# Selective-scan image kernel: the last stage of an image placed inside the next image's attention, x kept raw and updated in place, v computed in three row bands

## The chip, the cores and the metric

The kernel runs on one core of one Trainium2 chip. The metric is device time in microseconds (us) of the whole launch. Before the change three runs took 21485.61, 21488.65 and 21491.22 us; the median is 21488.65 us. All values are 32-bit floats.

## The reference, cut to what matters

Eight images of 384 channels by 64x64 pixels pass through two residual layers. Layer 0 is channel attention on a group-normalized input, layer 1 a four-direction selective scan with a token layer norm and a gelu.

```
xn   = group_norm(x)                                # 32 groups of 12 channels
q,k,v = dwconv3x3(conv1x1(xn, w*), dw*)             # 1x1 mix of channels, then a 3x3 depthwise filter
attn = softmax(l2norm(q) @ l2norm(k).T * temp)      # 8 heads of 48 channels, over the 4096 pixels
x    = x + conv1x1(attn @ v, wproj)
y    = selective_scan(group_norm(x))                # 4 directions, state of 16 per channel
x    = x + gelu(layer_norm_over_channels(y) * ln_w + ln_b)
```

## The kernel before, in words

Channels lie on the 128 partitions, in NJ = 3 blocks (j or m); the 4096 pixels of a row lie in the free dimension, in eight chunks of 512. One loop over the images (L789) calls three functions in turn; each opens its own pools of on-chip memory and closes them.

**channel_attention (L138).** Three tiles xn of 128x4096 are loaded (L153), their statistics taken (L168) and turned into mean and rstd per channel by norm_factors (L103: two groups of one-column matmuls and a few tiny vector operations). VectorE then normalizes xn in place (L171). conv (L175) makes one 128x4096 block of k, q or v: per chunk three accumulating matmuls into a PSUM tile pc of three buffers (L182), a ScalarE copy into pre (L186), then one ScalarE multiply by the centre tap (L187) and eight VectorE multiply-adds, one per other tap (L197), each over the whole block. pre and acc have two buffers each. inverse_norm (L203) squares a block with its sum on ScalarE (L205), then a square root and two tiny vector operations. to_tokens (L211) turns a block into tokens by matmuls against the identity (L215; for k against diag(1/norm), so that k is scaled on the way) and ScalarE copies (L219). q's tokens are multiplied with k's into pa (L246), from which the logits (L251), softmax (L255 to L260) and the merged matrix mT = attention times wproj (L267, L271) follow. v (L273) shares its memory with kT. When all of v stands, 24 blocks of 128x512 are projected (L287), added to x, which is loaded a second time (L282, L292), measured for the next group norm (L293) and stored to x1d in DRAM (L294).

**selective_scan (L297).** After norm_factors and a normalization in place (L336 on ScalarE, L341 on VectorE) it runs 32 steps of 8 periods each. In a period VectorE runs six scans (L481), GpSimd two products (L469), ScalarE exponentials (L462) and copies (L515), TensorE transposes and sums (L503, L538, L544); B comes by DMA (L416), three periods ahead. All of these are pinned to their written order. The sums go to y in DRAM (yd, L570, L589).

**finish (L746).** All of y is loaded as tokens (L756) and measured (L762, L763), normalized on VectorE (L771), transposed back (L779), passed through gelu (L782), added to x1 on GpSimd (L786, xr loaded at L769) and stored (L787). o and xr have two buffers.

What is not pinned is ordered by a scheduler when the program is built: it fixes one static order for each engine and for each queue of DMA issues, by program order and expected readiness. Each engine works through its own order strictly. A tile tag with n buffers makes the tile n allocations later wait until the earlier one has been read for the last time. The PSUM pool ps_m of the attention has one buffer, tag "misc".

Of the kernel before, what the change touches and what calls it, by code (L numbers as in the profile page):

```python
# [9 lines left out]
F32 = mybir.dt.float32  # L10
AF = mybir.ActivationFunctionType
# [4 lines left out]
P = 128  # L16
# [18 lines left out]
PX = 4  # L35
GN_EPS = 1e-5
# [35 lines left out]
def tile_channel_attention_then_selective_scan(ctx: ExitStack, tc: tile.TileContext, a: dict):  # L72
# [12 lines left out]
    nc.vector.tensor_add(pair, twos[:, :, 0], twos[:, :, 1])  # L85
    eps = const.tile([P, 1], F32, name="eps")
# [16 lines left out]
    def norm_factors(pool, psum, stats, tag, bank):  # L103

        avg = pool.tile([P, NJ, C], F32, name=f"avg{tag}")
# [32 lines left out]
    def channel_attention(b):  # L138

        with ExitStack() as st:  # L140
# [7 lines left out]
            xn = []  # L148
            for j in range(NJ):
                t = big.tile([P, L], F32, tag="x", bufs=NJ, name=f"xn{b}_{j}")  # L150
                for h in range(2):
                    eng = nc.sync if h == 0 else nc.scalar
                    eng.dma_start(t[:, bass.ts(h, L // 2)], x_d[b, j, :, bass.ts(h, L // 2)])  # L153
                xn.append(t)
            wts, dws = {}, {}
            for n in ("wk", "wq", "wv", "wproj"):
                wts[n] = wp.tile([P, NJ, C], F32, name=f"{n}{b}")
                nc.sync.dma_start(wts[n], a[n].rearrange("(j p) o -> p j o", p=P))
            for n in ("dwk", "dwq", "dwv"):
                dws[n] = wp.tile([P, NJ, 9], F32, name=f"{n}{b}")  # L160
                nc.scalar.dma_start(dws[n], a[n])
            mask = wp.tile([P, NJ, BW], F32, name=f"mask{b}")
            nc.scalar.dma_start(mask, a["mask"])

            stats = wp.tile([P, NJ, NCH, nc.vector.BN_STATS_DIM], F32, name=f"st0{b}")
            for j in range(NJ):
                for c in range(NCH):
                    nc.vector.bn_stats(stats[:, j, c, :], xn[j][:, bass.ts(c, CH)])  # L168
            mean, rstd = norm_factors(wp, ps_m, stats, f"0_{b}", "misc")
            for j in range(NJ):  # L170
                nc.vector.tensor_scalar(  # L171
                    xn[j], xn[j], mean[:, j : j + 1], rstd[:, j : j + 1], ALU.subtract, ALU.mult
                )

            def conv(which, m, acc):  # L175

                wt, dw = wts["w" + which], dws["dw" + which]
                pre = work.tile([P, L], F32, tag="pre", name=f"pre{b}{which}{m}")
                for c in range(NCH):
                    pc = ps_c.tile([P, CH], F32, tag="pc", name=f"pc{b}{which}{m}_{c}")  # L180
                    for j in range(NJ):
                        nc.tensor.matmul(  # L182
                            pc, lhsT=wt[:, j, m * P : (m + 1) * P], rhs=xn[j][:, bass.ts(c, CH)],
                            start=j == 0, stop=j == NJ - 1,
                        )
                    nc.scalar.copy(pre[:, bass.ts(c, CH)], pc)  # L186
                nc.scalar.activation(acc, pre, AF.Copy, scale=dw[:, m, 4:5])  # L187
                pre3 = pre.rearrange("p (h w) -> p h w", w=W)
                acc3 = acc.rearrange("p (h w) -> p h w", w=W)
                for tap in range(9):  # L190
                    if tap == 4:
                        continue
                    dy, dx = tap // 3 - 1, tap % 3 - 1
                    y0, y1 = max(0, -dy), H - max(0, dy)
                    x0, x1 = max(0, -dx), W - max(0, dx)
                    o = acc3[:, y0:y1, x0:x1]
                    nc.vector.scalar_tensor_tensor(  # L197
                        o, pre3[:, y0 + dy : y1 + dy, x0 + dx : x1 + dx],
# [4 lines left out]
            def inverse_norm(acc, junk, tag):  # L203
                r = work.tile([P, 1], F32, tag="rn", name=f"rn{tag}")
# [6 lines left out]
            def to_tokens(acc, rhs, t4, out, tag):  # L211

                pt = ps_t.tile([P, 4, P], F32, tag="pt", name=f"pt{tag}_{t4}")
                for i in range(4):
                    nc.tensor.matmul(  # L215
                        pt[:, i, :], lhsT=acc[:, bass.ts(4 * t4 + i, P)], rhs=rhs,
                        start=True, stop=True,
                    )
                nc.scalar.copy(out, pt)  # L219

            kT = wp.tile([P, NT, C], F32, tag="kv", name=f"kT{b}")
            for m in range(NJ):
                acc = work.tile([P, L], F32, tag="acc", name=f"ak{b}{m}")
                pre = conv("k", m, acc)
                r = inverse_norm(acc, pre, f"k{b}{m}")
                diag = work.tile([P, P], F32, tag="diag", name=f"diag{b}{m}")
                nc.vector.tensor_scalar_mul(diag, ident, r)
                for t4 in range(NT // 4):
                    to_tokens(acc, diag, t4, kT[:, 4 * t4 : 4 * t4 + 4, bass.ts(m, P)], f"k{b}{m}")

            attn = wp.tile([P, NJ, C], F32, name=f"attn{b}")
            nc.gpsimd.memset(attn, 0.0)
            for m in range(NJ):
# [3 lines left out]
                pre = conv("q", m, acc)  # L237
# [3 lines left out]
                for t4 in range(NT // 4):  # L241
                    qT = work.tile([P, 4, P], F32, tag="qT", name=f"qT{b}{m}_{t4}")
                    to_tokens(acc, ident, t4, qT, f"q{b}{m}")
# [6 lines left out]
                lg = work.tile([P, BW], F32, tag="lg", name=f"lg{b}{m}")  # L250
                nc.vector.scalar_tensor_tensor(  # L251
                    lg[:, :wd], pa[:, :wd], r, mask[:, m, :wd], ALU.mult, ALU.add
# [8 lines left out]

            mT = wp.tile([P, NJ, C], F32, name=f"mT{b}")
            for j in range(NJ):
                pm = ps_a.tile([P, CH], F32, tag="pa", name=f"pmt{b}{j}")
                src = [i for i in range(NJ) if _overlaps(i, j)]
                for i in src:
                    nc.tensor.matmul(  # L267
                        pm[:, :C], lhsT=attn[:, i, bass.ts(j, P)], rhs=wts["wproj"][:, i, :],
# [5 lines left out]
            for m in range(NJ):  # L274
                conv("v", m, v[:, m, :])

            x1 = []
            x1_d = dram.tile([NJ, P, L], F32, tag="x1d", bufs=2, name=f"x1d{b}")
            stats1 = big.tile([P, NJ, NCH, nc.vector.BN_STATS_DIM], F32, tag="st1", name=f"st1{b}")
            for m in range(NJ):  # L280
# [561 lines left out]
```

## Time and profile before

| what | value |
|---|---|
| median of 3 runs | 21488.65 us |
| span of the profiled execution | 21487.3 us |
| VectorE (DVE) busy | 19284.7 us, 90% |
| TensorE (PE) busy | 19225.0 us, 89% |
| ScalarE (ACT) busy | 17613.4 us, 82% |
| GpSimd (POOL) busy | 15773.4 us, 73% |
| one image, from the end of one scan to the end of the next (image 1) | 2682.3 us |
| of it the scan | 2104.1 us |
| of it finish, attention and the start of the scan | 578.2 us |

In the profile's map of 40 equal slices each image is five slices: VectorE is over 90% busy in the three or four that are scan, 70% in the first, which holds the end of one image and the attention of the next. Idle time of an engine is shown ahead of the instruction that ended it, with the engine or transfer that released it in brackets. Times inside image 1 are given from the start of the span; its predecessor's scan ends at 2612.0 us.

### The profile page before, as it was taken

The page shows a single profiled execution, that of the slowest core. Times are in us where ns is not written, and L with a number is a line of the kernel's source. Part 1 is how long each engine was busy: PE and PEld are TensorE (multiplying, and loading weights), DVE is VectorE, ACT ScalarE, POOL GpSimd, SP SyncE. Part 2 cuts the span into 40 slices and gives each one's busy share as a digit, 9 for nine tenths or more (in the row PEclk, how much of TensorE's full clock was granted, in tenths as well). Part 3 has the DMA queues.
Part 4 walks back from the last instruction along what each step waited for, and adds up shares of the span by engine and source line. Part 5 has one row for each costly group of instructions (what it writes and reads, how often), then busy time and mean ns, then how long its engine had stood idle before and what let it go on. Part 6 is the DMA issues. An engine that isn't in the chain of part 4 may idle for free. (4 is left out here: it accounts for less than half of the span.)

```text
span 21487.3 us, 318562 instructions
## 1 busy us (share of the span) xinstructions
PE 19225.0 (89%) x118832; PEld 10739.5 (50%) x118832; DVE 19284.7 (90%) x16862; ACT 17613.4 (82%) x30794; POOL 15773.4 (73%) x7117
## 2 busy tenths in 40 slices
PE   7999879998799987999879998799987999879998
PEld 4555445554455544555445554455544555445554
DVE  7999879998799987999879998799987999879998
ACT  3999839998399983999839998399983999839998
POOL 0999809998099980999809998099980999809998
PEclk8999989999899998999989999899998999989999
DMA  1222312223122231222312223122231222312223
GB/s 50 80 91 91 115 45 80 91 91 116 43 80 90 92 117 42 80 90 91 118 41 81 90 91 118 41 81 90 91 119 41 80 90 92 119 40 81 90 92 107
DMA packets 871616, 1807.88 MB, mean 84 GB/s; under 512 B 123216, under 2 KB 512592, under 8 KB 860848
## 3 DMA queue, kind: packets, MB, share of 16 engines
q1 hardware_dynamic: 807888, 1658.85, 24.0%
q10 hardware_dynamic: 62176, 128.66, 1.7%
q8 instruction: 936, 15.34, 0.3%
q14 instruction: 616, 5.05, 0.1%
HBM read 1468.39 MB, written 318.77 MB: 83 GB/s over the span
## 5 line engine op out<-in xcount | busy, mean ns | idle before, releaser
L469 POOL TENSOR_TENSOR db<-w,B 128x1536 f32<-128x1536 f32 x4096 | 14157.7, 3464 | 393.0 <-DVE h L481 213.8
L481 DVE TENSOR_TENSOR_SCAN h<-da,ca,db 128x512 f32<-128x512 f32 x10752 | 13075.0, 1267 | 642.3 <-ACT da L462 317.1
L515 ACT ACTIVATE hc<-pt,ct 128x384 f32<-128x384 f32 x15128 | 8533.2, 580 | 438.9 <-PE pt L503 342.6
L462 ACT ACTIVATE da<-dt,neg_a 128x512 f32<-128x512 f32 x12288 | 8511.9, 696 | 112.7 <-DVE h L481 80.8
L503 PE MATMUL pt<-ident,h 128*128 128x128 f32 x49152 | 8076.3, 288 | 517.7 <-ACT hc L515 345.7
L503 PEld LDWEIGHTS pt<-ident,h 128*128 128x128 f32 x49152 | 5140.4, 141 | 5154.1 <-ACT hc L515 2548.5
L538 PE MATMUL py<-hc,pair 128*64 128x384 f32 x24576 | 5329.1, 512 | 9.1 <-DVE ys L589 9.1
L446 POOL TENSOR_TENSOR w<-x,dt 128x512 f32<-128x512 f32 x768 | 1083.7, 1412 | 3884.9 <-DMA cx<-bcd 3884.9
L544 PE MATMUL py<-hc,pair 128*64 128x128 f32 x24576 | 2114.2, 281 | 0.0
L481 DVE TENSOR_TENSOR_SCAN h<-da,db 128x512 f32<-128x512 f32 x1536 | 1814.4, 1231 | 246.6 <-ACT da L462 105.4
L538 PEld LDWEIGHTS py<-hc,pair 128*64 128x64 f32 x24576 | 1216.1, 135 | 1014.3 <-issue 944.9
L544 PEld LDWEIGHTS py<-hc,pair 128*64 128x64 f32 x24576 | 1568.5, 137 | 208.7 <-issue 130.2
L370 PE MATMUL px<-x,wx 128*44 128x128 f32 x6144 | 1477.1, 338 | 35.1 <-ACT x L336 28.9
L370 PEld LDWEIGHTS px<-x,wx 128*44 128x44 f32 x6144 | 645.5, 121 | 815.7 <-issue 750.6
L495 POOL COPY ca<-h 128x6 f32<-128x6 f32 x1792 | 345.7, 193 | 905.5 <-DVE h L481 902.1
L429 PE MATMUL pd<-xd,wdt 128*128 128x512 f32 x1536 | 780.0, 617 | 73.9 <-ACT hc L515 61.1
L517 DVE TENSOR_SCALAR hc<-pt,ct 128x384 f32<-128x384 f32 x1256 | 734.0, 600 | 54.9 <-PE pt L503 25.4
L134 ACT ACT_TABLE_LOAD x16 | 20.5, 1283 | 913.9 <-DVE rstd L133 841.7
L287 PE MATMUL pp<-v,mT 128*128 128x512 f32 x1152 | 525.4, 618 | 272.9 <-DVE v L197 272.9
L786 POOL TENSOR_TENSOR o<-o,xr 128x512 f32<-128x512 f32 x192 | 310.5, 1646 | 510.9 <-DVE y L771 385.1
L779 PE MATMUL pz<-ident,y 128*128 128x128 f32 x768 | 152.3, 374 | 474.6 <-DVE y L771 293.4
L287 PEld LDWEIGHTS pp<-v,mT 128*128 128x128 f32 x1152 | 226.4, 198 | 570.5 <-issue 532.2
(238 smaller groups left out, 11677.0 us busy)
## 6 DMA issues: line engine op xcount, KB each, us to landing
B<-bcd SPq DMA_DIRECT2D x2048, 512.0 KB
yd<-ys SPq DMA_DIRECT2D x128, 576.0 KB
ys<-yd SPq DMA_DIRECT2D x256, 288.0 KB
yd<-ys SPq DMA_DIRECT2D x256, 288.0 KB
x<-in_x SPq DMA_DIRECT2D x24, 2048.0 KB
x1d<-x ACTq DMA_DIRECT2D x192, 256.0 KB
y<-yd SPq DMA_DIRECT2D x64, 768.0 KB
xr<-x1d ACTq DMA_DIRECT2D x64, 768.0 KB
```

Of the source, the lines that this page charges most:

```text
L287: nc.tensor.matmul(pc, lhsT=mT[:, j, bass.ts(m, P)], rhs=v[:, j, bass.ts(c, CH)], start=j == 0, stop=j == NJ - 1,)
L370: pin(nc.tensor.matmul(split(pxs[s][:XR, :])[:, part, :], lhsT=wx[:, j, k, :], rhs=view(x1[j], k, c)[:, part, :], start=i == 0, stop=i == ...
L429: pin(nc.tensor.matmul(pds[j], lhsT=wdt[:, k, bass.ts(j, P)], rhs=xds[s], start=True, stop=True))
L446: pin(nc.gpsimd.tensor_mul(split(ws[s][:, j, :]), view(x1[j], k, c), split(dts[s][:, j, :])))
L462: pin(nc.scalar.activation(t, dts[s][:, j, :], AF.Exp, scale=neg_a[:, j, k, n : n + 1]))
L469: pin(nc.gpsimd.tensor_mul(t, ws[g // NP], bts[g][:, v : v + 1, :].broadcast_to([P, NJ, CH])))
L481: pin(nc.vector.tensor_tensor_scan(h, da, db, 0.0 if start else carries[s - 1][:, j, n : n + 1], ALU.mult, ALU.add,))
L503: pin(nc.tensor.transpose(t[:, bass.ts(j, P)], h2s[g][:, j, bass.ts(q, HP), :].rearrange("p l v -> p (l v)"), ident))
L515: pin(eng.activation(out, src, AF.Copy, scale=scale))
L517: pin(eng.tensor_scalar_mul(out, src, scale))
L538: pin(nc.tensor.matmul(py[f * HP : (f + 1) * HP, lb, :C], lhsT=pair, rhs=hc[:, f, :], **flags))
L544: pin(nc.tensor.matmul(py[f * HP : (f + 1) * HP, j, C:], lhsT=pair, rhs=hc[:, f, bass.ts(j, P)], **flags,))
```

## The change

- **The end of image b moves into the attention of image b+1.** finish is left for the last image alone. Its statistics become token_norm (16 loads of 256 tokens through three buffers), its rest finish_part, 16 parts of 256 tokens: one y load, one x1 load, two ScalarE operations that normalize, six transposes in the PSUM tag "pt", three gelus of 256 columns, one VectorE add of 128x768 (GpSimd has none any more), one store. A part takes a buffer of the tag "acc" (two of them), which k and q used before. Two parts are written after each block of v.
- **x is loaded by load_x**, written after the second period of the last step of the scan, and only by SP. Attention reads it raw: the weights are scaled by rstd on ScalarE, and minus weights times mean, a bias made by nine one-column matmuls into "misc", is added where ScalarE empties a chunk. xn's normalization and the second load of x are gone; the projection is added to x in place. The weights and the averaging matrix share two buffers ("wt"), so each is loaded when a buffer comes free.
- **k's first block is made in two halves of 32 rows, v in three bands of 32, 16 and 16 rows**; a band takes one more row on either side, for v an "edge" row kept from the band before. After a band is complete for all three blocks its projections are written among the next band's.
- **k's tokens are no longer scaled.** They are transposed at once; the inverse norms are spread to all partitions by a matmul of ones with diag (into "misc") as rks, and multiplied into the logits by one more VectorE operation per block of q.
- All attention DMAs, x1d's stores among them, are issued by SP.

```diff
-    def norm_factors(pool, psum, stats, tag, bank):
-        avg = pool.tile([P, NJ, C], F32, name=f"avg{tag}")
+    def norm_factors(pool, psum, stats, tag, bank, home={}):
+        avg = pool.tile([P, NJ, C], F32, name=f"avg{tag}", **home)
...
+    def load_x(b):
+        xs = []
+        for j in range(NJ):
+            t = big.tile([P, L], F32, tag="x", bufs=NJ, name=f"x{b}_{j}")
+            for h in range(2):
+                nc.sync.dma_start(t[:, bass.ts(h, L // 2)], x_d[b, j, :, bass.ts(h, L // 2)])
+            xs.append(t)
+        return xs
...
-            for j in range(NJ):
-                nc.vector.tensor_scalar(
-                    xn[j], xn[j], mean[:, j : j + 1], rstd[:, j : j + 1], ALU.subtract, ALU.mult
-                )
+            def weights(which):
+                wt = load_w("w" + which)
+                for j in range(NJ):
+                    nc.scalar.activation(wt[:, j, :], wt[:, j, :], AF.Copy, scale=rstd[:, j : j + 1])
+                pb = ps_m.tile([P, CH], F32, tag="misc", name=f"pb{b}{which}")
+                for m in range(NJ):
+                    for j in range(NJ):
+                        nc.tensor.matmul(
+                            pb[:, m : m + 1], lhsT=wt[:, j, bass.ts(m, P)], rhs=mean[:, j : j + 1],
...
+                bias = wp.tile([P, NJ], F32, name=f"bias{b}{which}")
+                nc.scalar.activation(bias, pb[:, :NJ], AF.Copy, scale=-1.0)
+                return wt, bias
...
-                    nc.scalar.copy(pre[:, bass.ts(c, CH)], pc)
-                nc.scalar.activation(acc, pre, AF.Copy, scale=dw[:, m, 4:5])
+                    nc.scalar.activation(
+                        pre[:, o : o + n], pc[:, :n], AF.Identity, bias=bias[:, m : m + 1]
+                    )
+                o = (y0 - lo) * W
+                nc.scalar.activation(
+                    out, pre[:, o : o + (y1 - y0) * W], AF.Copy, scale=dw[:, m, 4:5]
+                )
...
+            wk, bk = weights("k")
...
             for m in range(NJ):
                 acc = work.tile([P, L], F32, tag="acc", name=f"ak{b}{m}")
-                pre = conv("k", m, acc)
+                parts = (0, H // 2, H) if m == 0 else (0, H)
+                for y0, y1 in zip(parts, parts[1:]):
+                    pre = conv("k", wk, bk, m, y0, y1, acc[:, y0 * W : y1 * W])
                 r = inverse_norm(acc, pre, f"k{b}{m}")
                 diag = work.tile([P, P], F32, tag="diag", name=f"diag{b}{m}")
                 nc.vector.tensor_scalar_mul(diag, ident, r)
+                pr = ps_m.tile([P, CH], F32, tag="misc", name=f"pr{b}{m}")
+                nc.tensor.matmul(pr[:, :P], lhsT=ones, rhs=diag, start=True, stop=True)
+                nc.scalar.copy(rks[:, bass.ts(m, P)], pr[:, :P])
...
+            wq, bq = weights("q")
...
+            wv, bv = weights("v")
+            emit = None
+            if before is not None:
+                scale, shift = token_norm(b, wp, work, before[2])
+                def emit(i):
+                    t = work.tile([P, L], F32, tag="acc", name=f"fin{b}_{i}")
+                    room = [t[:, n * FT * NJ : (n + 1) * FT * NJ] for n in range(3)]
+                    finish_part(*before, i, scale, shift, room, ps_t, "pt")
...
-            for m in range(NJ):
-                conv("v", m, v[:, m, :])
...
-                t = big.tile([P, L], F32, tag="x", bufs=NJ, name=f"x1{b}_{m}")
-                nc.sync.dma_start(t, x_d[b, m])
...
+            parts = (0, H // 2, 3 * H // 4, H)
+            todo, left, edges = [], list(range(L // FT)) if emit else [], {}
+            for y0, y1 in zip(parts, parts[1:]):
+                for m in range(NJ):
+                    pre = conv("v", wv, bv, m, y0, y1, v[:, m, y0 * W : y1 * W], edges.get(m))
...
+                    if m > 0:
+                        for _ in range(min(len(todo), 6)):
+                            project_out(*todo.pop(0))
+                    for _ in range(min(len(left), 2)):
+                        emit(left.pop(0))
+                todo += [(m, c) for c in range(y0 * W // CH, y1 * W // CH) for m in range(NJ)]
+            for t in todo:
+                project_out(*t)
...
             for g in range(S * NP + 1):
                 period(g)
+                if g == (S - 1) * NP + 1 and b + 1 < B:
+                    x_next = load_x(b + 1)
...
+    def finish_part(b, x1_d, y_d, i, scale, shift, room, psum, tag):
...
+        nc.vector.tensor_add(o, o, xr)
+        nc.sync.dma_start(out_d[b, :, :, cs].rearrange("j p l -> p j l"), o)
...
+    x, before = load_x(0), None
     for b in range(B):
-        x1, x1_d, stats1 = channel_attention(b)
-        y_d = selective_scan(b, x1, stats1)
-        finish(b, x1_d, y_d)
+        x1, x1_d, stats1 = channel_attention(b, x, before)
+        y_d, x = selective_scan(b, x1, stats1)
+        before = (b, x1_d, y_d)
+    finish(*before)
```

## The prediction, on record before the changed kernel ran

> **What bounds the kernel now.** I read three views of image 1 in this order. First the table of stretches, cut at the stage borders: stretch, its length, then busy time of each engine with its instructions, PE clock, DMA share and rate.
>
> ```profile
> core 0: us, PE busy (x) PEld busy (x) DVE busy (x) ACT busy (x) POOL busy (x), PEclk, DMA share, GB/s
> 2612.00:2698.70 86.70, 18.79 (x96) 15.56 (x96) 31.30 (x98) 19.84 (x27) 38.81 (x24) 0.58 0.67 227
> 2698.70:2751.90 53.20, 34.18 (x87) 18.21 (x88) 23.09 (x36) 9.88 (x12) 1.06 (x1) 0.71 0.18 62
> 2751.90:2996.40 244.50, 203.31 (x878) 127.97 (x877) 213.61 (x80) 106.28 (x132) 0.00 (x0) 0.92 0.00 0
> 2996.40:3101.50 105.10, 47.04 (x100) 19.62 (x98) 104.64 (x26) 18.44 (x22) 0.00 (x0) 0.74 0.15 60
> 3101.50:3163.00 61.50, 59.09 (x140) 26.64 (x140) 35.06 (x53) 0.00 (x0) 0.00 (x0) 0.97 0.32 117
> 3163.00:3190.20 27.20, 15.34 (x76) 12.18 (x76) 10.56 (x29) 12.92 (x17) 7.12 (x5) 0.75 0.18 67
> 3190.20:5294.30 2104.10, 2024.77 (x13480) 1121.24 (x13480) 1992.14 (x1789) 2033.83 (x3642) 1924.44 (x861) 1.00 0.28 89
> ```
>
> The scan (last row) has four engines over 91% busy; its pinned order is untouched, so I leave its time alone. Of the other 578.2 us, DVE binds k, q (third row, 87%) and v (fourth, 99.6%), PE the projection (fifth); in finish and start (140 us) nobody is busy. Second, the timeline of DVE, for the gap before each stage (start, length, idle and releaser):
>
> ```profile
> 2698.68 14.34 DVE L168 BATCH_NORM_STATS2 st<-xn 128x6 f32<-128x512 f32 x24 [39.89 <-DMA out<-o]
> 2751.94 52.14 DVE L197 SCALAR_TENSOR_TENSOR ak<-pre1k,dwk,ak 128x3969 f32<-128x3969 f32 x12 [23.64 <-ACT ak L187]
> ...
> 2831.14 30.94 DVE L197 SCALAR_TENSOR_TENSOR ak<-pre1k,dwk,ak 128x3969 f32<-128x3969 f32 x7 [4.22 <-PE pc1q L182]
> ...
> 2992.66 0.37 DVE L251 SCALAR_TENSOR_TENSOR lg<-pa,rnq,mask 128x144 f32<-128x144 f32 x1 [12.78 <-PE pa L246]
> ...
> 3005.32 96.21 DVE L197 SCALAR_TENSOR_TENSOR v<-pre1v,dwv,v 128x3969 f32<-128x3969 f32 x22
> ```
>
> Between the first tap (2751.9) and q's last (2973.7) DVE stands only 9 us: blocks overlap. Third, the groups, for durations (busy, mean ns, idle before):
>
> ```profile
> L287 PE MATMUL pp<-v,mT 128*128 128x512 f32 x144 | 65.6, 617 | 34.0 <-DVE v L197 34.0
> L182 PE MATMUL pc1q<-xn,wq 128*128 128x512 f32 x144 | 65.2, 609 | 12.7 <-ACT pre1q L186 12.7
> L187 ACT ACTIVATE ak<-pre1k,dwk 128x4096 f32<-128x4096 f32 x3 | 11.1, 3713 | 0.1
> L205 ACT ACTIVATE pre1k<-ak 128x4096 f32<-128x4096 f32 x3 | 10.9, 3618 | 39.0 <-DVE ak L197 39.0
> L762 DVE BATCH_NORM_STATS2 fst<-y 128x6 f32<-128x384 f32 x32 | 16.1, 544 | 15.1 <-DMA xr<-x1d 12.7 <-DMA y<-yd 2.4
> ```
>
> ScalarE's copies of pc in the timeline show a chunk of a convolution every 2.57 us.
>
> **What the Trainium skill says.** "DMA: Bandwidth & Descriptors", section "Anatomy of one DMA", puts about 2 us of fixed cost on a DMA and says that waits happen on the issuing sequencer, not in the DMA engines: a store that waits for an add holds up every issue behind it on SP. The trace agrees: y's first load is issued at 2617.7, 5.7 us after yd's stores began. "ScalarE: Activation LUTs", section "Table sets: the hidden batching unit", says copy and identity are in every table set; so scaled weights and biased emptying add no table loads, only gelu among exponentials does, one per image (1283 ns each in the trace). "VectorE: DVE Perf Modes", section on the TRN2 errata, charges a fixed cost per instruction. Here 22 taps take 96.21 us, 4.373 each; by the difference of the two tap shapes (4416 less 4351 ns over 63 elements, 1.03 ns each) some 0.2 us of a tap is fixed. That prices the split taps: 2.29 us for half a block, 1.25 for a quarter.
>
> **The change part by part**, in us after the end of the preceding scan (2612.0 before). I follow the built program's static order, which is the same for images 1 to 7.
>
> *Start.* x is already loaded inside the scan before too (its last issues stand at 2602), so issue by SP alone costs nothing that I can see: at most 1 MB lies ahead of a B that is fetched three periods of 7.5 us early. Finish's 86.7 go; statistics start at 0, rstd stands at 22.5 as before, plus 1.5 for token statistics put between. Then three weight scalings at 0.47 (L271's row, 1.4), nine bias matmuls (2), four chunks and one row (11), emptying and half a centre tap (2.5): first tap at 41. Ahead of it stand 13 of 16 token statistics, 1.14 each; their loads go round three buffers at about 1.7 (estimated from a round trip of 5), and SP waits with wq for the averaging matrix's buffer, with token loads 4 to 15 queued behind it and these statistics ahead of the taps on DVE: 42 (38 to 47). Before: 139.9. **Gain 98.**
>
> *k and q.* Here the order gives back. (a) k0 takes 16 half taps, 36.6, and 3.4 of statistics: ends 82. On PE the last matmul of k1's convolution stands behind k0's second-half transposes and pr, which waits for square (3.6), root and diag: 5.3 to pr, 3 of transposes and matmul, 0.6 and 3.7 on ACT: k1 starts 13.5 later. (b) k1 and k2: 71. Then bias q: pb needs "misc", whose one buffer pr of k2 holds until rks is copied, so q's emptying waits for k2's norm; three chunks fill pc and PE stops. From k2's last tap: 6 to pr and rks, 2 transposes groups 2.2, pb 2, transposes and v's pb 6, five chunks 12.9, emptying and centre tap 4.3: **33 of idle DVE**. (c) q0 and q1: 71; q2 waits, as before, 32.6 from q0's square to its centre tap, and since q0 and q1 are now interleaved alone, DVE waits 14. (d) q2 and its small operations 36.7. Sum: 42+40+13.5+71+33+71+14+36.7 = 321; the token copies end 17.5 later as before: 338.5. Before: 379.2 (2991.2). So the idle 60.5 in place of 9, and 6 of statistics and splits, leave **41 of the 98**.
>
> *v and tail.* Before, from that point to the last statistics: 171.7. Now DVE does taps 55 + 60 = 115 (before 105), eighteen projections' adds and statistics at 1.38 (25), sixteen adds of 768 at 1.0 (0.69 for 512 from PSUM, scaled; 16), then six projections at PE's 2.57 (15 of 62). Sum with 3 for the first logits: 174. PE has about 118 in this window: conv 66, 18 projections 46, 96 transposes 32, less some 26 done ahead. Where v's third block of a band waits behind projections and part transposes, I count stalls of 2, 4, 2 and 2 us; the parts' adds have 17 us between pairs, but 7 between parts 11 and 12, where a store, a load and gelu (about 12) miss by 5, which partly overlap: 11 in all. 185, so **13 lost** (bounds 4 and 35; lower than 4 is excluded by the sum). Each store waits on SP for its add; behind it stand the next part's load and x1d's stores, and nobody waits for the latter before the scan's normalization. ACT's 65 (28 for the convolution, 20 to normalize, 22 gelus less overlap) and POOL's vacated adds do not bind. x's second load and xn's normalization are gone; the former was hidden behind v, the latter's 7 us is in the start's gain.
>
> *Sum.* Images 1 to 7: 41 - 13 = 28 each, 196. Image 0 has no parts: first tap 18.6 earlier (50 for 68.6), then the same idle, so q ends 34 later; v and tail 161 for 172: 23 lost. The last finish is divided finer, its loads doubled: 13 lost (0 to 30). -196 + 23 + 13 = -160 on the span of 21487.3: 21327; its run and the others lie within 4 us, so the median is taken as **21330 us**.
>
> **The rivals.** *A: the gaps don't open.* If a, b and c together stay at the 9 us of before, all eight images gain 51 more: 21330 - 410 = 20920. For it: before, blocks overlap. Against: "misc" and PE's fixed order. *B, slower: the two "acc" buffers.* Part i+2 loads only when part i is stored, and DVE, in order, stands at the add. Before, chunks of finish with two o buffers took 5 us each with 227 GB/s over the stage, which speaks for slow round trips. With a pair every 28 us: 10 + 7x28 + 23 = 229, 57 over 171.7; 57 - 41 = 16, times 7, plus 36: 21635. It turns the sign above some 25 us a pair; I estimate 15 to 17, hidden by taps. *C: DMA and PE together stretch v by 26*: 7x(26-41)+36 = -69: 21418. For it: parts, x1d's stores and y's second reading put five passes over 6 MB into v's 185 us (about 130 GB/s, where finish reached 227), and PE's last blocks stand between part transposes. Against: neither is near its own limit. *The change doesn't do what it says:* statistics could still wait for pools; the order puts them right behind the scan's last adds, which excludes it.
>
> **How the numbers follow.** Likeliest 0.73, A 0.10, C 0.08, B 0.09. The range, 21140 to 21460, takes gaps 25 us shorter per image below, and C and the v bound above; A and B stay out. About 0.2% (43 us) is what measurement tells from no change. Below 21446: most of the likeliest, A and most of C, 0.85; within, 0.06; slower, B and a tail, 0.09.
>
> **What would show it.** First tap about 42 after a scan; DVE idle of about 13, 33 and 14 before k1, q0 and q2, ended by ACT's centre taps; DVE busy 85% or more in v's stretch, down from 99.6%; no gap at the parts' adds over 6 us. Wrong if q0's gap is under 15 (A), or adds wait for "out" over 10 us a pair (B).

## The result, and the profile after

The changed kernel takes 21297.12 us, the median of four runs (21290.69 to 21307.95); beside it the kernel before takes 21489.94 (21485.61 to 21495.37). The ratio is 0.9911, with a 95% interval of 0.9893 to 0.9928: 193 us gained, where 160 were predicted. The profiled spans are 21288.9 and 21487.3. The period of an image, from the last addition of one scan to that of the next, fell from 2683.9 to 2649.3 on the mean of seven: 34.6 less each, 242 in all. Image 0 lost 30.7 us, the last finish 12.8. The sum is 198.4, the difference of the two spans.

First the table of stretches of image 1 of the changed kernel, cut at the end of the preceding scan (2642.7), the first tap of k, the ends of the gap before q0, the first logits of q2, the last statistics and the first step of the next scan. Columns: stretch, length, busy time of each engine with its instructions, TensorE clock, DMA share and rate.

```profile
core 0: us, PE busy (x) PEld busy (x) DVE busy (x) ACT busy (x) POOL busy (x), PEclk, DMA share, GB/s
2642.70:2691.70 49.00, 24.13 (x82) 15.90 (x83) 31.05 (x86) 9.79 (x15) 1.06 (x1) 0.65 0.61 183
2691.70:2812.20 120.50, 71.91 (x207) 36.76 (x205) 109.27 (x52) 41.45 (x52) 0.00 (x0) 0.80 0.02 7
2812.20:2848.50 36.30, 33.93 (x111) 22.91 (x112) 0.60 (x3) 17.69 (x24) 0.00 (x0) 0.72 0.00 0
2848.50:2987.70 139.20, 100.92 (x434) 67.47 (x433) 108.11 (x46) 54.45 (x72) 0.00 (x0) 0.85 0.04 12
2987.70:3161.30 173.60, 136.28 (x385) 63.52 (x383) 157.96 (x145) 73.89 (x126) 0.00 (x0) 0.90 0.43 144
3161.30:3188.90 27.60, 15.84 (x76) 12.35 (x76) 10.63 (x29) 12.91 (x17) 7.15 (x5) 0.72 0.19 67
3188.90:5292.10 2103.20, 2024.27 (x13480) 1121.46 (x13480) 1992.31 (x1789) 2034.09 (x3642) 1923.78 (x860) 1.00 0.27 89
```

The scan, in the last row, is as long as it was (2103.2 for 2104.1). Finish and start, 139.9 us together before, are now the 49.0 of the first row. The third row is new: 36.3 us in which VectorE works for 0.6. The fifth holds v, the projection and the final stage of the image before; VectorE is busy in 91% of it, and its 173.6 us stand against 170.2 for v and projection before. Next the timeline of VectorE in the same image: start, length, instruction, and in brackets the idle time before it and what ended that.

```profile
2648.32 14.34 DVE L169 BATCH_NORM_STATS2 st<-x 128x6 f32<-128x512 f32 x24 [5.65 <-DMA yd<-ys]
...
2691.66 2.25 DVE L237 SCALAR_TENSOR_TENSOR ak<-pre1k,dwk,ak 128x1953 f32<-128x1953 f32 x1 [1.88 <-ACT ak L225]
2742.28 52.15 DVE L237 SCALAR_TENSOR_TENSOR ak<-pre1k,dwk,ak 128x3969 f32<-128x3969 f32 x12 [6.56 <-ACT ak L225]
2848.53 52.14 DVE L237 SCALAR_TENSOR_TENSOR aq<-pre1q,dwq,aq 128x3969 f32<-128x3969 f32 x12 [31.46 <-ACT aq L225]
2932.28 13.19 DVE L237 SCALAR_TENSOR_TENSOR aq<-pre1q,dwq,aq 128x3969 f32<-128x3969 f32 x3 [6.10 <-ACT aq L225]
2987.66 0.31 DVE L297 TENSOR_TENSOR lg<-pa,rks 128x144 f32<-128x144 f32 x1 [13.46 <-PE pa L292]
...
3081.35 1.27 DVE L237 SCALAR_TENSOR_TENSOR v<-pre1v,dwv,v 128x1008 f32<-128x1008 f32 x1 [3.23 <-ACT v L225]
3103.87 7.74 DVE L237 SCALAR_TENSOR_TENSOR v<-pre1v,dwv,v 128x1008 f32<-128x1008 f32 x6 [3.54 <-ACT v L225]
3135.57 10.23 DVE L237 SCALAR_TENSOR_TENSOR v<-pre1v,dwv,v 128x1008 f32<-128x1008 f32 x8 [1.58 <-ACT v L225]
3148.03 0.69 DVE L343 TENSOR_TENSOR x<-x,pp 128x512 f32<-128x512 f32 x1 [2.23 <-PE pp L338]
```

The brackets count idle time since any instruction, and a norm's tiny operations break some gaps up. From last tap to first tap the three gaps are 11.7 us before k1, 36.3 before q0 and 14 before q2. The first line shows a wait that no step of the prediction has: the statistics of x start 5.65 us after the scan, when the last store of y has landed. Third, four groups of image 1 (busy time, mean ns, idle before):

```profile
L338 PE MATMUL pp<-v,mT 128*128 128x512 f32 x144 | 67.9, 623 | 14.5 <-DVE v L237 7.2 <-ACT pre1v L221 6.4 <-DVE x L343 0.9
L216 PE MATMUL pc1q<-x,wq 128*128 128x512 f32 x144 | 64.6, 603 | 0.0
...
L830 DVE BATCH_NORM_STATS2 fst<-fy 128x6 f32<-128x384 f32 x32 | 16.5, 544 | 5.1 <-DMA fy<-yd 5.1
...
L858 DVE TENSOR_TENSOR fin<-fin 128x768 f32<-128x768 f32 x16 | 15.2, 953 | 0.5 <-ACT fin L854 0.5
```

The projection's idle time fell from 34.0 to 14.5: it no longer stands behind the whole of v. Token statistics wait for loads 5.1 us where they waited 15.1, and the sixteen additions of the parts wait half a microsecond in all.

### The profile page after: what moved, and what is told of

It is laid out like the page before. It is cut to its first block, busy times and chain, and to the rows that moved or that the text cites. A ratio compares the mean times of both kernels' runs of the same rounds, so it can differ in the third digit from the quotient of the medians.

```text
span 21288.9 us, 318429 instructions
## 1 busy us (share of the span) xinstructions
PE 19267.7 (91%) x118160; PEld 10725.5 (50%) x118160; DVE 19285.1 (91%) x17190; ACT 17955.0 (84%) x31571; POOL 15456.3 (73%) x6926
## 5 line engine op out<-in xcount | busy, mean ns | idle before, releaser
L255 PE MATMUL ptk<-ident,ak 128*128 128x128 f32 x768 | 163.9, 382 | 373.2 <-DVE ak L237 336.8
L509 ACT ACTIVATE dt<-pd,dt_bias 128x512 f32<-128x512 f32 x768 | 476.2, 687 | 24.9 <-PE pd L499 21.3
L499 PEld LDWEIGHTS pd<-xd,wdt 128*128 128x128 f32 x1536 | 275.1, 192 | 388.5 <-issue 187.1
```

The costliest lines, as they stand in the source:

```text
L499: pin(nc.tensor.matmul(pds[j], lhsT=wdt[:, k, bass.ts(j, P)], rhs=xds[s], start=True, stop=True))
```

## The experiments

Each kernel was timed beside the kernel before, whose medians were 21484 to 21492 (e9 and e10 on another chip, where it was 21491.5); times are compared with the changed kernel's 21297. "After the scan" is counted from the end of image 1's preceding scan. In some images of a kernel the first tap comes 3 to 5 us later than in its other images. Image 1 is such a late image in e1 and in e4 to e10, and an early one in the changed kernel and e2. The last section says more about it.

**e1: q's bias before k.**

```diff
             wk, bk = weights("k")
+            wq, bq = weights("q")
...
-            wq, bq = weights("q")
             attn = wp.tile([P, NJ, C], F32, name=f"attn{b}")
```

> The changed kernel with one line moved: q's weights are loaded and scaled, and q's bias is made, ahead of k's blocks, so that pb of q takes the one bank of "misc" before the pr's of k's norms; all sums are the same. Theory (q0's first tap waits because pb of q stands behind pr of k2 in "misc"): the gap on VectorE before q0's first tap falls from 36 us to 4 to 12, the gaps before k1 (12) and q2 (14) stay, all eight images gain 24 to 32: 190 to 255 us under the changed kernel's 21297, so 21040 to 21105. Rival (the two "pre" buffers, or the order of the transposes on TensorE, hold q0): the gap stays at 25 or more, and the time stays within 60 us of 21297.

Measured: 21101.99 us, ratio to before 0.9823 (0.9809 to 0.9838). From the timeline of VectorE of e1, the first taps of k0 and of q0:

```profile
2679.84 2.25 DVE L237 SCALAR_TENSOR_TENSOR ak<-pre1k,dwk,ak 128x1953 f32<-128x1953 f32 x1 [7.72 <-ACT ak L225]
...
2804.93 4.35 DVE L237 SCALAR_TENSOR_TENSOR aq<-pre1q,dwq,aq 128x3969 f32<-128x3969 f32 x1 [4.49 <-ACT aq L225]
```

The gap before q0 is 4.5 us for 36.3, and the others stayed (12.2 and 14.8). So what held q0 is q's bias standing behind k's norms. That the one bank of "misc" puts it there, and not TensorE's order alone, is argued from the program: no run gave "misc" a second bank. The first tap moved from 49.0 to 56.2 after the scan in image 1 (54.0 to 54.8 in five of the other six), as q's nine bias matmuls and scalings now stand ahead of k0; so an image gains 24.

**e2: k scaled in the matmul, as before the change.**

```diff
-                    nc.tensor.transpose(pt[:, i, :], acc[:, bass.ts(4 * t4 + i, P)], ident)
+                    nc.tensor.matmul(pt[:, i, :], lhsT=acc[:, bass.ts(4 * t4 + i, P)], rhs=rhs, start=True, stop=True)
...
-                pr = ps_m.tile([P, CH], F32, tag="misc", name=f"pr{b}{m}")
-                nc.tensor.matmul(pr[:, :P], lhsT=ones, rhs=diag, start=True, stop=True)
-                nc.scalar.copy(rks[:, bass.ts(m, P)], pr[:, :P])
...
-                nc.vector.tensor_mul(lg[:, :wd], pa[:, :wd], rks[:, lo:hi])
```

> The changed kernel with one part of the change undone: k's tokens are again scaled by the diagonal in the matmul that transposes them; the ones matmul pr, the row rks and the product of the logits with it are gone. Nothing but q and v's biases then asks for "misc", and nothing of k's norms stands ahead of k1's or q0's convolution on TensorE. Theory: both gaps close, that before k1 (12 us) and that before q0 (36 us), to under 8 us each or 10 to 12 in all; 36 to 38 us in each of eight images, so about 21000 (20970 to 21030). Rival (the gap before k1 comes from k0 being made in two halves, which hold both "pre" buffers, and not from pr): only q0's gap closes, 21040 to 21105.

Measured: 21022.1 us, ratio 0.9787 (0.9773 to 0.9802). The first taps of k1 and q0 in e2:

```profile
2707.16 8.81 DVE L237 SCALAR_TENSOR_TENSOR ak<-pre1k,dwk,ak 128x3969 f32<-128x3969 f32 x2 [3.84 <-ACT ak L225]
...
2778.29 4.35 DVE L237 SCALAR_TENSOR_TENSOR aq<-pre1q,dwq,aq 128x3969 f32<-128x3969 f32 x1 [0.74 <-ACT aq L225]
```

The time is what the theory said, but not all of its parts: q0's gap is 0.7, k1's is still 8.8 us from tap to tap (its bracket shows only the piece after the norm's reciprocal), over the bound of 8. In TensorE's order of e2 no transpose stands ahead of k1's chunks any more, so something else holds k1; the rival had named the two "pre" buffers, which e9 tries. From the first logits of q2 to the last statistics e2 takes 179.7 us, 6 more than the changed kernel. The traces show where: v's taps wait 12.2 us for ScalarE in place of 9.2, the projections' additions 6.9 for TensorE in place of 4.8, the parts' additions 1.4 in place of 0.5. Image 0, without parts, takes 169.7 and 169.5. What delays ScalarE there was not tried.

**e3: the statistics' tile in another pool.**

```diff
-            stats = wp.tile([P, NJ, NCH, nc.vector.BN_STATS_DIM], F32, name=f"st0{b}")
+            stats = big.tile([P, NJ, NCH, nc.vector.BN_STATS_DIM], F32, tag="st0", name=f"st0{b}")
```

> The changed kernel with the tile of attention's first statistics in the pool of x, which lives through all images, in place of attention's own pool, whose memory was the scan's. Theory (statistics wait 5.65 us for yd's last store, because their tile lies where ys lay; and everything behind them is later by that): the wait goes, first tap 43 to 44 us after the scan in place of 49; seven images gain 5 each: 35 under 21297, about 21262. Rival (the loads of the final stage's tokens, which start behind the same store, set the first tap in any case): the wait at the statistics goes, but the waits at the tokens' statistics grow by about as much, and the time stays within 15 us of 21297.

Measured: 21344.05 us, ratio 0.9935 (0.9921 to 0.995): 47 slower, which neither expected. From the timeline of VectorE of e3, within the scan and at its end:

```profile
2533.77 0.69 DVE L169 BATCH_NORM_STATS2 st<-x 128x6 f32<-128x512 f32 x1 [0.21 <-DMA x<-in_x]
...
2554.24 1.29 DVE L169 BATCH_NORM_STATS2 st<-x 128x6 f32<-128x512 f32 x2 [1.52 <-DMA x<-in_x]
...
2664.49 0.83 DVE L113 BATCH_NORM_AGGREGATE mv<-st 128x2 f32<-128x48 f32 x3 [5.67 <-DMA yd<-ys]
```

With its memory free, the scheduler put the 24 statistics into the scan, 125 to 70 us before its end, between scan steps, where VectorE is busy for 95% of the time. The first tap comes 40.4 us after the scan, 8.6 earlier, but the period is 2656.2 for 2649.0 (mean of images 1 to 6): the scan takes 2119.0 us in place of 2103.2 in image 1, and 2101.8 in image 7, which has no next image's statistics to take in. The wait passed to the next tile of attention's own pool, mv. The late start of the statistics had kept 14.3 us of work out of an almost full engine.

**e4: no final stage in attention.**

```diff
-            if before is not None:
+            if before is not None and b < 0:
```

> The changed kernel without the final stage of images 0 to 6: their token statistics and the 16 parts are left out of the next attention, so that seven eighths of the output are not written. It prices what attention carries. The prediction counted, in the start, 13 of 16 token statistics at 1.14 us (15) ahead of the first tap, and 3 in k0 (3.4); in v, 16 us of adds and 11 of stalls; 45 us an image. Theory (the parts cost what VectorE spends on them and nothing more, since load, gelu and store are hidden): start 30 to 34 us to the first tap, v and tail 154 to 160 from the first logits of q2 in place of 173.6, so 32 to 38 us less an image: 21297 - 7 x 35 = 21050 (21030 to 21075). Rival (the parts cost more than their instructions, by the ring of two "acc" buffers, by the queue of SP or by the DMA engines that they share with the stores): v and tail under 150, an image 45 or more: under 20985.

Measured: 21277.54 us, ratio 0.9905 (0.9888 to 0.9921): 20 less than the changed kernel, where some 250 and over 310 were expected. Both fell. From the timeline of VectorE of e4, the first tap and the waits for ScalarE in v's last bands:

```profile
2701.51 4.57 DVE L237 SCALAR_TENSOR_TENSOR ak<-pre1k,dwk,ak 128x1953 f32<-128x1953 f32 x2 [22.48 <-ACT ak L225]
```

```profile
3088.25 1.27 DVE L237 SCALAR_TENSOR_TENSOR v<-pre1v,dwv,v 128x1008 f32<-128x1008 f32 x1 [5.58 <-ACT v L225]
3109.42 14.59 DVE L237 SCALAR_TENSOR_TENSOR v<-pre1v,dwv,v 128x1008 f32<-128x1008 f32 x12 [4.40 <-ACT v L225]
...
3142.14 10.23 DVE L237 SCALAR_TENSOR_TENSOR v<-pre1v,dwv,v 128x1008 f32<-128x1008 f32 x8 [5.64 <-ACT v L225]
```

Without any token statistics VectorE stands for 22.5 us from the reciprocal of rstd to the first tap in image 1, which is late (first tap at 52.2), and for 18.5 in images 3 and 4, which are early (48.3 and 48.4). In the changed kernel, with token statistics, the same way takes 18.1 to 18.6 us in its early images. So scaling, bias, chunks and centre tap take that time in any case, and the token statistics fit into it. In v the three waits are 5.6, 4.4 and 5.6 us; with the parts they were 3.2, 3.5 and 1.6. All waits of v's taps for ScalarE in image 1 add up to 17.8 us, and to 9.2 with the parts. From the first logits of q2 to the last statistics it is 169.7 us for 173.6: the 15.2 us of additions cost 4.

The difference of 20 us hides a part of the price, because five of e4's seven images are late and only one of the changed kernel's. In images 3 and 4, early in both, the period is 2641.8 and 2641.9 us for 2649.1 and 2648.8. So the parts cost 7 us an image: 4 in v and tail and 3 before the first logits of q2, where three token statistics still stand among k0's taps.

**e5: as e4, and v in one band.**

```diff
-            parts = (0, H // 2, 3 * H // 4, H)
+            parts = (0, H)
```

> The kernel of e4 (final stage of images 0 to 6 left out, seven eighths of the output not written) with v made in one band of 64 rows in place of three, so that all 24 projections come after v. It prices the bands without the parts; the comparison is with e4's 21278. Theory 1 (from the sums: taps 105 us in place of 115, but 62 of projections in place of 15 in the tail and 25 beside the taps): v and tail 167 to 174 us against e4's 169.7, because e4's taps wait for ScalarE's centre taps at each band; so within 40 us of 21278, and the bands are worth nothing by themselves. Theory 2 (the bands hide 18 projections at 2.57 us and cost 10 of taps): v and tail 195 to 210, eight images: 21480 to 21600.

Measured: 21310.81 us, ratio 0.9915 (0.99 to 0.993); v and tail take 172.5 us in image 1 and up to 174.9 in others. This is theory 1: by themselves the bands save 33 us in eight images. With the parts they leave waits in which sixteen additions find room; whether the parts would fit as well beside a single band was not tried.

**e6: six parts at a time.**

```diff
-                    for _ in range(min(len(left), 2)):
+                    for _ in range(min(len(left), 6)):
```

> The changed kernel with up to six parts of the final stage after each third of a band in place of two: the same work, but parts follow each other after some 6 us of VectorE (two to three taps and an add) in place of 17, so that the two "acc" buffers' round trip shows. Theory (the prediction's 15 to 17 us a pair, 8 a part): adds of twelve parts wait 1 to 2 us each, the last band has no parts to fill its waits (about 9 us): v and tail 173.6 + 15 to 30, and 21400 to 21510. Rival B's price (28 us a pair, 14 a part): 12 waits of 8, some 90 us an image: over 21850. Third: the round trip is shorter than 6 us: no wait over 0.5 at the adds, and only the waits in the last band come back: 21297 to 21370.

Measured: 21403.94 us, ratio 0.9959 (0.9944 to 0.9974), just within the theory's range; v and tail take 190.3 us. Six additions of parts in a row, from the timeline of VectorE of e6:

```profile
3060.93 0.96 DVE L858 TENSOR_TENSOR fin<-fin 128x768 f32<-128x768 f32 x1 [0.26 <-ACT fin L854]
3064.94 0.96 DVE L858 TENSOR_TENSOR fin<-fin 128x768 f32<-128x768 f32 x1 [0.82 <-ACT fin L854]
3075.34 0.96 DVE L858 TENSOR_TENSOR fin<-fin 128x768 f32<-128x768 f32 x1 [2.21 <-ACT fin L854]
3079.34 0.96 DVE L858 TENSOR_TENSOR fin<-fin 128x768 f32<-128x768 f32 x1
3086.73 0.95 DVE L858 TENSOR_TENSOR fin<-fin 128x768 f32<-128x768 f32 x1
3092.27 0.96 DVE L858 TENSOR_TENSOR fin<-fin 128x768 f32<-128x768 f32 x1 [2.21 <-ACT fin L854]
```

A part uses the buffer of the last but one. Where the addition waited longest, the two are 14.4 us apart (3060.93 to 3075.34) and 12.9 (3079.34 to 3092.27): that is the round trip of the two buffers, with whatever ScalarE did in between. It is half of rival B's 28 us, and under the 17 us that the prediction counted between pairs in the changed kernel, whose additions wait 0.5 us in all. The sixteen additions of e6 wait 5.6 us in all, not the 12 to 24 of its theory. The larger share of its 16.7 us is that v's taps wait 17.8 us for ScalarE again, as in e4: the last bands have no parts left to fill these waits.

**e7: e2 with k's tokens first in the pool.**

```diff
+            kT = wp.tile([P, NT, C], F32, tag="kv", name=f"kT{b}")
             stats = wp.tile([P, NJ, NCH, nc.vector.BN_STATS_DIM], F32, name=f"st0{b}")
```

> The kernel of e2 (k's tokens scaled in the matmul) with the tile of k's tokens made first in attention's pool, 48 KB a partition, so that the statistics, and the small tiles of their norm, lie elsewhere than on the scan's last sums. Theory (the 5.66 us that statistics wait for yd's last store come from the place of their tile): statistics begin within 1 us of the scan's end, are not drawn into the scan as in e3 (the memory is another of the scan's, or is free late), and the first tap comes 3 to 6 us earlier than e2's 48.9; 20 to 45 us under e2's 21022. Rival (the wait is for the scan's pool as a whole, whatever the place): the wait stays 5 to 6 us and the time within 15 us of 21022. Second rival (drawn into the scan as in e3): 30 to 90 us above 21022.

Measured: 21037.47 us, ratio 0.9789 (0.9772 to 0.9805). The statistics waited 5.65 us as before: the first rival is right about the wait, and its time is 15.4 us above e2's, at the edge of its 15. The first tap came 52.7 us after the scan for e2's 48.9, with the same work ahead of it. The last stretch before the first tap in the two kernels, e2 first:

```profile
core 0: us, PE busy (x) PEld busy (x) DVE busy (x) ACT busy (x) POOL busy (x), PEclk, DMA share, GB/s
...
2647.90:2659.50 11.60, 11.60 (x32) 5.54 (x33) 7.36 (x25) 5.05 (x7) 0.00 (x0) 1.00 0.80 243
```

```profile
core 0: us, PE busy (x) PEld busy (x) DVE busy (x) ACT busy (x) POOL busy (x), PEclk, DMA share, GB/s
...
2645.20:2660.60 15.40, 15.40 (x38) 7.76 (x39) 7.27 (x24) 5.03 (x7) 0.00 (x0) 0.79 0.65 201
```

The clock column tells: 1.00 all through, or 0.79 on the mean. More on it in the last section.

**e8: k's norms late.**

```diff
+                if m == 0:
+                    wq, bq = weights("q")
...
-                pr = ps_m.tile([P, CH], F32, tag="misc", name=f"pr{b}{m}")
-                nc.tensor.matmul(pr[:, :P], lhsT=ones, rhs=diag, start=True, stop=True)
-                nc.scalar.copy(rks[:, bass.ts(m, P)], pr[:, :P])
+                diags.append(diag)
...
                 pre = conv("q", wq, bq, m, 0, H, acc)
+                if m == 0:
+                    for i in range(NJ):
+                        pr = ps_m.tile([P, CH], F32, tag="misc", name=f"pr{b}{i}")
...
```

> The changed kernel with its row of k's norms kept, but late: the three pr's and their copies stand after q0's convolution in the program (three diag buffers in place of two), and q's bias is made after k0's convolution, not before it as in e1 (which cost 7 us ahead of the first tap). All sums are the same. Theory (pr's wait for the norm, on TensorE's fixed order, is what holds k1's last chunk, and "misc" what holds q0): first tap at 49, the gap before k1 falls from 12 to 4 to 9, that before q0 from 36 to 2 to 7; 33 to 42 us in each of eight images: 20960 to 21035. Rival (k1 is held by the transposes of k0's second half, which wait for its last tap whatever pr does): k1's gap stays 10 to 12, and 21035 to 21065.

Measured: 21059.55 us, ratio 0.9798 (0.9784 to 0.9813), in the rival's range. From the timeline of VectorE of e8, the first taps of k1 and q0:

```profile
2721.43 52.14 DVE L237 SCALAR_TENSOR_TENSOR ak<-pre1k,dwk,ak 128x3969 f32<-128x3969 f32 x12 [6.03 <-ACT ak L225]
...
2795.93 4.35 DVE L237 SCALAR_TENSOR_TENSOR aq<-pre1q,dwq,aq 128x3969 f32<-128x3969 f32 x1 [4.61 <-ACT aq L225]
```

From last tap to first tap q0's gap is 4.6 and k1's 11.3, as good as unchanged. So pr is not what holds k1. ScalarE's timeline in the changed kernel shows what may, around the end of k0 (VectorE's last tap of k0 ends at 2730.5):

```profile
2718.31 1.85 ACT L221 ACTIVATE pre1k<-pc1k,bias1k 128x512 f32<-128x512 f32 x3 [15.56 <-DVE ak L237]
...
2737.82 0.69 ACT L221 ACTIVATE pre1k<-pc1k,bias1k 128x512 f32<-128x512 f32 x1 [0.23 <-PE pc1k L216]
2738.54 3.71 ACT L225 ACTIVATE ak<-pre1k,dwk 128x4096 f32<-128x4096 f32 x1
```

ScalarE stands 15.6 us and begins to empty k1's chunks when a tap of k0 lets it: k0's two halves hold both "pre" buffers, and their taps are interleaved, so that the first half's buffer comes free only 12 us before k0 is done.

**e9: one buffer for both halves of k0.**

```diff
-                pre = work.tile([P, L], F32, tag="pre", name=f"pre{b}{which}{m}_{y0}")
                 first = lo
+                if pre is not None:
+                    first, lo = y0 + 1, 0
+                else:
+                    pre = work.tile([P, L], F32, tag="pre", name=f"pre{b}{which}{m}_{y0}")
...
-                    pre = conv("k", wk, bk, m, y0, y1, acc[:, y0 * W : y1 * W])
+                    pre = conv("k", wk, bk, m, y0, y1, acc[:, y0 * W : y1 * W], pre=pre)
```

> The changed kernel with one edit: the two halves of k0 share one "pre" buffer (the second half goes on where the first stopped, and makes no edge row again), so that the other buffer is free for k1. The sums are the same. Theory, formed on e2 and e8, where the gap before k1 was 8.8 and 11.4: what holds k1 is neither pr nor the transposes; k0's halves hold both "pre" buffers, so ScalarE begins to empty k1's chunks only when the first half's last tap is done, 12 us before k0 ends, and needs 8 chunks at 2.57 us. The gap before k1 falls from 11.7 to under 5, that before q0 stays at 36; 7 to 12 us in each of eight images: 21200 to 21240. Rival (TensorE's order or ScalarE's square hold k1 all the same): gap 8 to 12, and the time within 35 us of 21297.

Measured: 21197.97 us, ratio 0.9864 (0.9847 to 0.988): 99 under the changed kernel, 12.4 an image, 2 us beyond the theory's range. From the timeline of VectorE of e9, the last half taps of k0 and the first tap of k1:

```profile
2718.92 13.02 DVE L240 SCALAR_TENSOR_TENSOR ak<-pre1k,dwk,ak 128x1984 f32<-128x1984 f32 x4
2732.02 4.32 DVE L240 SCALAR_TENSOR_TENSOR ak<-pre1k,dwk,ak 128x3969 f32<-128x3969 f32 x1
...
2828.04 52.14 DVE L240 SCALAR_TENSOR_TENSOR aq<-pre1q,dwq,aq 128x3969 f32<-128x3969 f32 x12 [28.90 <-ACT aq L228]
```

There is no gap left before k1, so the second "pre" buffer is what held it; q0's gap stands (33.9 us, its bracket broken up by k2's norm).

**e10: e2 and e9 together.**

> e2 (k's tokens scaled in the matmul, no pr and no row of norms) with the edit of e9 as well. Theory: both gaps close, that before q0 by e2's edit and that before k1 by e9's; 5 to 9 us an image under e2's 21022: 20950 to 20985. Rival (without k1's gap the next wait, at q0 or q1, takes its place, since ScalarE and TensorE then set the pace of k): within 25 us of 21022.

Measured: 20992.52 us, ratio 0.9766 (0.9751 to 0.9781), the fastest of all: 2.3% under the kernel before, 1.4% under the changed one. It gains 30 over e2 where 37 to 72 were expected. From the timeline of VectorE of e10, the first tap of k2 and the first piece of q1:

```profile
2726.23 4.35 DVE L240 SCALAR_TENSOR_TENSOR ak<-pre1k,dwk,ak 128x3969 f32<-128x3969 f32 x1 [3.44 <-ACT ak L228]
...
2805.60 13.20 DVE L240 SCALAR_TENSOR_TENSOR aq<-pre1q,dwq,aq 128x3969 f32<-128x3969 f32 x3 [4.45 <-PE pc1q L219]
```

The gaps before k1 and q0 are gone, but others stand in their place: from tap to tap 8.1 us before k2 and 9.2 before q1. So theory and rival are each half right. A part of what is missing is late first taps: e10 has four late images of seven, e2 none. Its three early images take 2609.0 to 2611.9 us, 6 to 9 under e2's 2618, as the theory had it; its late ones take 2614.8 to 2617.6.

## Why the prediction held, step by step

- **Start.** Predicted first tap 42 us after the scan (38 to 47), measured 49.0: 91 gained for 98. The step that failed is "statistics start at 0": they start at 5.65, when y's last store has landed, and all behind them is late by that; the other 1.4 us are spread over the chain to the first tap. The step took the memory of attention's pool as free when the scan's last instruction on VectorE was done, and the prediction held a wait for pools excluded. It had read the figure itself, at another place: y's first load, 5.7 us after yd's stores began. e3 and e7 show the same wait at another tile of that pool and at another place in it, and none for a tile outside. Adding 1 us for token statistics ahead of the taps was wrong too, though small: e4 shows them hidden behind the chain from rstd.
- **(a) k1.** Predicted 13.5, measured 11.7; the size was right by luck, as its reason was wrong. Without pr ahead of it k1's gap is 11.3 (e8), without pr and transposes still 8.8 (e2), so these two explain 3 us at most; with one "pre" buffer for both halves it is gone (e9).
- **(b) q0.** Predicted 33, measured 36.3, and for the stated reason, q's bias behind k2's norm: e1 takes it to 4.5 by moving one line. In the changed kernel TensorE runs q's bias matmuls at 2819.6, close behind pr of k2 at 2817.4, and the 1290 records of TensorE ahead of a scan come in the same order in images 1 to 7. As said at e1, the share of "misc" in this was not tried by itself.
- **(c) q2.** Predicted 14, measured 14; not tried by itself. q2's last tap ends at 325.4 after the scan for 321, and the first logits of q2 keep 35.7 of the 91 gained where 41 of 98 were predicted.
- **v and tail.** Predicted 13 lost, measured 3.4, under the lower bound of 4. The term that was mis-sized is the 16 us of additions with 11 of stalls on top. The stalls are waits for ScalarE and TensorE; e4 has them without the parts, and the additions go into them instead of being added. Image 0, which has no parts, says the same: its v and tail take 169.5 us where the prediction had 161. So v without parts was priced 8 us too low, and the parts were priced at 24 in v where they cost 4. Over the whole attention they cost 7 an image (e4).
- **The sum.** For image 1 it is 91.0 - 55.3 - 3.4 = 32.3 gained where 98 - 57 - 13 = 28 was predicted, and 34.6 on the mean of seven. Image 0 lost 30.7 for 23, the last finish 12.8 for 13. The start's 7 us too little, v's 10 too few lost and image 0's 8 too many have different signs; 33 us are left on the whole, so that the total came this close is in part luck.
- **Slips in the working.** The parts listed under (a) add up to 12.6, not 13.5. The sum without stalls leaves 174 - 171.7 = 2 lost, so the bound of 4 does not follow from it. C's traffic is four passes over 6 MB, not five (144 GB/s in 173.6 us are 25 MB). A period of the scan is 8.2 us (2104.1 in 256), not 7.5. The result hangs on none of them.

Of the rivals, A was right that the gaps are worth much: without those of k1 and q0 e10 stands 305 under the changed kernel. But A's 20920 was not reached: new waits stand at k2 and q1, and the start is 7 us later than in A's sum. B's price was twice that of the round trip in e6 (28 for 14.4). C is not seen: DMA's share in the fifth stretch is 0.43, and v with its tail grew by 3.4.

## What to carry to other kernels

An engine that stands waiting in a stage takes added work for less than its duration (here 15.2 us of additions cost 4), so price added work against that stage's waits; the way to know is to leave it out. When a loop body is split to start earlier, count the buffers that the pieces hold: two halves in two buffers left none for the next block, and cost 12 us an image (e9). A small side computation (here the row of k's norms, with q's bias behind it in a pool of one buffer) can hold up a whole stage through an engine's fixed order (36 us an image, 4.5 after one line was moved).

## What was not expected of the hardware

The first tap comes at one of two times. In the nine traces whose start has the same work as the changed kernel's or less (all but e1 and e3), images 1 to 7 give 63 first taps: 37 come 47.9 to 49.1 us after the scan, 26 come 51.6 to 53.4. The changed kernel has one late image, e2 none, e4 five, e7 six, e10 four. The mean TensorE clock over the 12 us ahead of the first tap is 1.00 in all 37 early images and 0.86 to 0.93 in all 26 late ones. The Trainium skill, "TensorE: Matmul & The Clock Gate", in its Part 1 on the clock gate, says that a rested TensorE runs at half clock until a free-running window of about 3.4 us has been busy, and that where the window falls varies from run to run. The traces agree: the clock column is 0.50 over the 11 us in which the norm's matmuls run in the changed kernel, e2 and e7, and in one kernel the two times are 3 to 5 us apart. No run here moves the window.

In e4 the gap before q0 has two sizes too: it is 33.9 us at a mean clock of 0.78 in the early images and 37.3 to 37.5 at 0.70 or 0.71 in the late ones. A late image of e4 thus takes 6 to 8 us more than an early one, and the changed kernel's only late one 2 to 3 more. Five late images of e4 are then worth some 35 us, an estimate from these periods, more than the 20 between e4 and the changed kernel. So compare images of the same kind before a small difference between kernels is explained. Not every such difference is of this sort: e7's median is 15 us above e2's, but its profiled execution, with six late images, is 4 us shorter than e2's, which has none; e7's v and tail take 2 us an image less, and the four runs of e2 lie 26 us apart. Why is not known.

The other is the wait for the store. The Trainium skill's "DMA: Bandwidth & Descriptors", section "Anatomy of one DMA", puts most of the fixed 2 us of a DMA that GpSimd issues on the receipt of its last byte. The stores here are issued by SyncE. What waits for the last of them went on 5.65 us after the addition that filled its buffer (5.64 to 5.68 in image 1 of all eleven traces with the change, of which four stores' issue takes 2.85 in the changed kernel); how much of the rest is receipt no run here shows. Which of the scan's tiles holds attention's pool until then stays open.
